# Closing stage of a four-layer graph network: GpSimd arithmetic removed from the last loop, statistics kept in SBUF, weights folded and five batches loaded while the last batch ends

## The chip, the core and the metric

The kernel runs on one core of a Trainium2 chip. The metric is device microseconds for one launch: the median of three runs of the kernel before is 2222.99 us (2221.63 to 2226.77). A core has five engines with a queue each: TensorE (PE, matrix products; its weight loads are shown as PEld), VectorE (DVE), ScalarE (ACT), GpSimd (POOL) and SyncE (SP). An engine takes the instructions of its queue in order. DMA transfers are issued from the queues of SP, ACT and POOL; an issue holds its queue until what it waits for has come.

## The reference

Sixteen graphs (batches) of 1024 nodes with 64 channels, a 1024 x 1024 adjacency matrix each, go through four layers. Each layer ends in "add to the input, then normalise over the channels". Layers 0 to 2 are a graph convolution, a Chebyshev graph filter and a quantile aggregation over neighbours with a small perceptron. The stage that is changed belongs to layer 3:

```python
Hf = H.reshape(batch * l, c)
mean = Hf.mean(axis=0)
var = jnp.mean((Hf - mean) ** 2, axis=0)
Hn = ((Hf - mean) * jax.lax.rsqrt(var + BN_EPS) * gamma + beta).reshape(batch, l, c)
d = A.sum(axis=2)
A_norm = jnp.sqrt(d)[:, :, None] * A * jax.lax.rsqrt(d)[:, None, :]
A_hat = jnp.eye(l, dtype=A.dtype) - A_norm
X = Hn @ W + b
out = jnp.einsum('bij,bjo->bio', A_hat, X)
return jax.nn.leaky_relu(out, negative_slope=0.01)
...
x = _layernorm(x + _L3_gnn_ref(x, adj, L3_gnn_gamma, L3_gnn_beta, L3_gnn_W, L3_gnn_b), axis=-1)
```

The mean and the variance run over the nodes of all sixteen batches. So nothing of the last product with `W` can be finished before the last batch has its layer-2 output, and the kernel needs a closing loop over the batches.

## The kernel before

The main phase works on the sixteen batches as a software pipeline. Each batch is a set of Python generators (`rows_in`, `layers`, `lists`, `fetch`, `heads`, `sorts`, `ends`, `back`, `third`), each with a table of due times in `WHEN`, and a new batch starts every `PERIOD` (120) units. All steps are sorted by due time and emitted in that order under a manual schedule; so the order on every engine's queue is written out by hand, and the engines only wait for semaphores.

`third` is the last generator of a batch. Its step "again" loads the transposed adjacency back (four transfers of 1 MB). Its step "u" (index 1) turns the layer-2 output `f_x3t` on PE, copies it on ACT (L1006), stores it to DRAM (`x3_d`, L1007), takes the batch-norm statistics on DVE (L1009) and stores those to DRAM in two small transfers (`st_d`, L1011), then scales by 1/sqrt(degree) on ACT (L1014, L1015). Its step "sum" is the product with the adjacency (`hop2`, L464: 16 matmuls of fp32, 32 passes on PE). The last two steps scale, subtract and store the result `z` (`z_d`, L1038).

After the main phase a flag is computed (L1083 to L1088): was there any node for which the fast path is not valid? Every engine loads the flag into a register (L1092) and branches (L1094) past a fallback that computes all batches in another way. The fallback is not taken with these inputs. The branch target is the closing stage.

The closing stage first folds: it loads the statistics of all batches from DRAM (`sts`, L1645) and gamma, beta, `W` and bias (L1647 to L1654), aggregates (L1656), forms 1/sqrt(var + eps) on ACT (L1658) and a small matrix `left` on DVE, multiplies it with `W` on PE (L1674), and writes the result twice into a block-diagonal matrix `w_2` (L1681). Then the closing loop treats each batch in seven steps, again under a manual schedule, with a lag in batches for each step:

```python
for t in range(-2, B + 3):
    for step, late in ((centre, 2), (finish, 3), (residual, 1), (square, 2), (mean, 1), (root, 2), (product, -2)):
        if 0 <= t - late < B:
            step(t - late)
```

`product` loads `z` (SP queue) and `x3` (ACT queue), 256 KB each, and multiplies `z` with `w_2` (L1694). `residual` is the leaky rectifier (ACT L1700, DVE L1701), the residual addition (DVE L1703) and the sum over channels (DVE L1705). `centre` subtracts the mean on POOL (L1713), `square` squares on ACT and sums on DVE (L1717, L1719), `root` is a square root on ACT (L1723), `finish` a reciprocal on DVE (L1727), a product on POOL (L1729) and the store of the batch's output from SP (L1730).

Of the kernel before, what the change touches and what calls it, by code (L numbers as in the profile page):

```python
# [218 lines left out]
def gnn_layers_kernel(  # L219
# [64 lines left out]
    st_d = dpool.tile([B, C, 12], F32, name="st_d")  # L284
# [41 lines left out]
    flag_i = cpool.tile([P, 1], I32, name="flag_i")  # L326
    stack = ExitStack()
# [484 lines left out]
    def heads(b, st, gots, pw, ps_):  # L812

        meta, xs = st["meta"], st["xs"]
        for ns, nr, _, ks in CLASSES:
# [38 lines left out]
            home = ps_.tile([P, HOME], F32, name="home", bufs=2)[:, 0 : ns * nk * C].rearrange(  # L854
# [141 lines left out]
    def third(b, st, pa, pw):  # L996
# [11 lines left out]
        st = pw.tile([P, 6], F32, name="f_st")  # L1008
        nc.vector.bn_stats(out=st, in_=xt)  # L1009
        for h in range(2):  # L1010
            nc.sync.dma_start(out=st_d[b][:, h * 6 : h * 6 + 6], in_=st[h * C : (h + 1) * C, :])  # L1011
# [27 lines left out]
        yield "z"  # L1039

    with (
# [23 lines left out]
        for b in range(B):  # L1065
            st = {}
            for name, part in (
                ("rows in", rows_in(b, st, keyband, pa, pw)),
                ("layers", layers(b, st, pw)),
                ("lists", lists(b, st, pw)),  # L1070
                ("fetch", fetch(b, st, gots)),
                ("heads", heads(b, st, gots, pw, ps_)),
                ("sorts", sorts(b, st, ps_)),
                ("ends", ends(b, st, pw)),
                ("back", back(b, st, pw)),
                ("third", third(b, st, pa, pw)),
            ):
                parts += [(b * PERIOD + when, b, name, u, part) for u, when in enumerate(WHEN[name])]
        for _, b, name, u, part in sorted(parts, key=lambda p: p[0]):
            next(part)  # L1080

        most = fc.tile([P, 1], F32, name="most")
        nc.vector.tensor_reduce(out=most, in_=missed, axis=AX.XY, op=ALU.max)  # L1083
        most_h = fc.tile([P, 1], BF16, name="most_h")
        nc.vector.tensor_scalar(out=most_h, in0=most, scalar1=0.0, scalar2=None, op0=ALU.is_gt)
        ps = bank("end")
        nc.tensor.matmul(ps[:, 0:1], lhsT=ones_h, rhs=most_h, start=True, stop=True)
        nc.vector.tensor_scalar(out=flag_i, in0=ps[:, 0:1], scalar1=0.0, scalar2=None, op0=ALU.is_gt)  # L1088
# [4 lines left out]
    with (  # L1093
# [40 lines left out]
        with tc.For_i(0, B, 1) as b:  # L1134
# [128 lines left out]
            with (  # L1263
                tc.tile_pool(name="l2", bufs=1) as l2,
                tc.tile_pool(name="l2d", bufs=2) as l2d,
# [315 lines left out]
            with tc.tile_pool(name="post", bufs=1) as post:  # L1581
# [34 lines left out]
                nc.sync.dma_start(out=st_d[bass.ds(b, 1)].rearrange("o c s -> c (o s)"), in_=st.rearrange("c f s -> c (f s)"))  # L1616
# [26 lines left out]
    with tc.tile_pool(name="fin1", bufs=1) as fin1, tc.tile_pool(name="fin", bufs=4) as fin, tc.tile_pool(name="ps_small", bufs=6, space=PSUM) as psum["small"]:  # L1643
        sts = fin1.tile([C, B, 12], F32, name="sts")
        nc.sync.dma_start(out=sts, in_=st_d.rearrange("b c s -> c b s"))  # L1645
        gam = fin1.tile([C, 2], F32, name="gam")
        nc.scalar.dma_start(out=gam[:, 0:1], in_=gamma.rearrange("(c o) -> c o", o=1))  # L1647
        nc.scalar.dma_start(out=gam[:, 1:2], in_=beta.rearrange("(c o) -> c o", o=1))
        w3_s = fin1.tile([C, C], F32, name="w3_s")
        nc.scalar.dma_start(out=w3_s, in_=w3)  # L1650
        b3_s = fin1.tile([P, C], F32, name="b3_s")
        nc.vector.memset(b3_s, 0.0)
        for h in range(2):
            nc.scalar.dma_start(out=b3_s[h * C + C - 1 : h * C + C, :], in_=b3.rearrange("(o c) -> o c", o=1))  # L1654
        mv = fin1.tile([C, 2], F32, name="mv")
        nc.vector.bn_aggr(out=mv, in_=sts.rearrange("c b s -> c (b s)"))  # L1656
        rs = fin1.tile([C, 1], F32, name="rs")
        nc.scalar.activation(rs, mv[:, 1:2], AF.Sqrt, bias=eps_s[0:C, :], scale=1.0)  # L1658
        nc.vector.reciprocal(rs, rs)
        nc.vector.tensor_tensor(out=rs, in0=rs, in1=gam[:, 0:1], op=ALU.mult)  # L1660

        left = fin1.tile([C, P], F32, name="left")
        shifts = fin1.tile([C, 1], F32, name="shifts")
        nc.vector.tensor_tensor(out=shifts, in0=mv[:, 0:1], in1=rs, op=ALU.mult)
        nc.vector.tensor_tensor(out=shifts, in0=gam[:, 1:2], in1=shifts, op=ALU.subtract)
        for h in range(2):
            cols = slice(h * C, (h + 1) * C)
            nc.vector.tensor_tensor(
                out=left[:, cols], in0=ident[0:C, 0:C], in1=ident[0:C, C - 1 : C].to_broadcast([C, C]), op=ALU.subtract
            )  # L1670
            nc.vector.tensor_scalar(out=left[:, cols], in0=left[:, cols], scalar1=rs, scalar2=None, op0=ALU.mult)
            nc.vector.tensor_copy(out=left[:, h * C + C - 1 : h * C + C], in_=shifts)
        ps = small()
        nc.tensor.matmul(ps[:, 0:C], lhsT=left, rhs=w3_s, start=True, stop=True)  # L1674

        w_2 = fin1.tile([P, P], F32, name="w_2")
        nc.vector.memset(w_2, 0.0)
        nc.vector.tensor_tensor(out=b3_s, in0=ps[:, 0:C], in1=b3_s, op=ALU.add)
        for h in range(2):
            hp = slice(h * C, (h + 1) * C)  # L1680
            nc.vector.tensor_scalar(out=w_2[hp, hp], in0=b3_s[hp], scalar1=-1.0, scalar2=None, op0=ALU.mult)  # L1681

# [3 lines left out]
        def product(b):  # L1686
            z = fin.tile([P, 512], F32, name="zf")
            nc.sync.dma_start(out=z, in_=z_d[b])  # L1688
            x3 = fin.tile([P, NK, C], F32, name="x3f", bufs=6)
            nc.scalar.dma_start(out=x3, in_=x3_d[b].rearrange("p (k c) -> p k c", c=C))  # L1690
# [4 lines left out]
            st[b].update(ps=ps, x3=x3)  # L1695

        def residual(b):
            psv = st[b]["ps"].rearrange("p (k c) -> p k c", c=C)
            low = fin.tile([P, NK, C], F32, name="low")
            nc.scalar.activation(low, psv, AF.Copy, scale=0.01)  # L1700
            nc.vector.tensor_tensor(out=psv, in0=low, in1=psv, op=ALU.max)  # L1701
            h = fin.tile([P, NK, C], F32, name="hf")
            nc.vector.tensor_tensor(out=h, in0=psv, in1=st[b]["x3"], op=ALU.add)  # L1703
            s = fin.tile([P, NK], F32, name="s")
            nc.vector.tensor_reduce(out=s, in_=h, axis=AX.X, op=ALU.add)  # L1705
            st[b].update(h=h, s=s)

        def mean(b):
            nc.scalar.mul(st[b]["s"], st[b]["s"], -1.0 / C)

        def centre(b):
            h, s = st[b]["h"], st[b]["s"]
            nc.gpsimd.tensor_tensor(out=h, in0=h, in1=s.unsqueeze(2).to_broadcast(wide), op=ALU.add)  # L1713

        def square(b):
            q = fin.tile([P, NK, C], F32, name="qf")
            nc.scalar.activation(q, st[b]["h"], AF.Square)  # L1717
            v = fin.tile([P, NK], F32, name="v")
            nc.vector.tensor_reduce(out=v, in_=q, axis=AX.X, op=ALU.add)  # L1719
# [5 lines left out]
        def finish(b):  # L1725
            r = fin.tile([P, NK], F32, name="r")
            nc.vector.reciprocal(r, st[b]["v"])  # L1727
            y = fin.tile([P, NK, C], F32, name="yf")
# [38 lines left out]
```

## Time and profile before

| | |
|---|---|
| three runs | 2226.77, 2222.99, 2221.63 us; median 2222.99 |
| profiled execution, its own time | 2229.29 us |
| its span, first to last instruction | 2227.4 us |
| mean granted TensorE clock | 0.871 |
| busy in the span | PE 1671.2 us (75%), DVE 1864.1 us (84%), ACT 1484.5 us (67%), POOL 1734.7 us (78%) |
| product with the adjacency of the last batch begins | 2126.60 us |
| last `z` copied (ACT L1037) | 2140.86 us, 0.59 us long |
| first product of the closing loop | 2154.60 us |
| last store of the output issued | 2221.65 us |
| engines at work after 2147 us | DVE 49.15, POOL 32.73, PE 30.51, ACT 26.50 of 80 us |

All times in the text are counted from the first instruction of this span. A line of the timeline gives the start, the duration, the engine, the line of the kernel and the operation, then the shapes, and in brackets how long the engine had been idle and what ended that. A "q" after an engine's name means its instruction queue: DMA issues, branches and waits. Busy shares over the whole span say little here, since all of the change lies in the last 100 us and in one step per batch before them.

### The profile page before, as it was taken

The page shows a single profiled execution, that of the slowest core. Times are in us where ns is not written, and L with a number is a line of the kernel's source. Part 1 is how long each engine was busy: PE and PEld are TensorE (multiplying, and loading weights), DVE is VectorE, ACT ScalarE, POOL GpSimd, SP SyncE. Part 2 cuts the span into 40 slices and gives each one's busy share as a digit, 9 for nine tenths or more (in the row PEclk, how much of TensorE's full clock was granted, in tenths as well). Part 3 has the DMA queues.
Part 4 walks back from the last instruction along what each step waited for, and adds up shares of the span by engine and source line. Part 5 has one row for each costly group of instructions (what it writes and reads, how often), then busy time and mean ns, then how long its engine had stood idle before and what let it go on. Part 6 is the DMA issues. An engine that isn't in the chain of part 4 may idle for free. (4 is left out here: it accounts for less than half of the span.)

```text
span 2227.4 us, 35713 instructions
## 1 busy us (share of the span) xinstructions
PE 1671.2 (75%) x9926; PEld 935.9 (42%) x9926; DVE 1864.1 (84%) x5687; ACT 1484.5 (67%) x5397; POOL 1734.7 (78%) x2279
## 2 busy tenths in 40 slices
PE   4876788878788778878788778878787877755653
PEld 3443444444445344444435344444444443333333
DVE  7658989889898989989898989999998988677536
ACT  3544767768686767768685767768686766675523
POOL 0078989899989989978787978889888979888014
PEclk9988889889899999989899998989998988876675
DMA  4444253533435353533535353533435352231226
GB/s 148 167 112 130 72 186 92 167 97 109 155 87 177 92 194 82 173 98 99 161 87 174 91 193 83 174 96 118 145 85 181 97 183 75 57 105 26 82 81 158
DMA packets 130481, 272.42 MB, mean 122 GB/s; under 512 B 77025, under 2 KB 77281, under 8 KB 120033
## 3 DMA queue, kind: packets, MB, share of 16 engines
q1 hardware_dynamic: 57536, 218.90, 27.2%
q0 software_dynamic: 35840, 37.92, 10.4%
q10 hardware_dynamic: 36896, 13.23, 2.4%
q8 instruction: 80, 1.31, 0.2%
q14 instruction: 129, 1.05, 0.2%
HBM read 185.89 MB, written 84.07 MB: 121 GB/s over the span
## 5 line engine op out<-in xcount | busy, mean ns | idle before, releaser
L803 POOL DMA_INDIRECT got<-rows,ids x1072 | 1139.7, 1063 | 186.0 <-issue 125.0
L806 POOL MEMSET rest<- 128x384 f32 x1120 | 509.4, 455 | 0.6
L464 PE MATMUL ps_l<-f_adj_t,f_t 128*64 128x512 f32 x1536 | 359.0, 622 | 35.5 <-ACT f_t L603 35.5
L875 ACT ACTIVATE home<-got,big 128x64 f32<-128x64 f32 x1344 | 329.9, 334 | 0.0
L907 DVE TENSOR_TENSOR away<-home 128x768 f32<-128x768 f32 (+9 forms) x416 | 228.9, 572 | 43.6 <-PE ps_xt L924 34.5
L924 PE MATMUL ps_xt<-home,quarter 128*128 128x256 f32 (+2 forms) x672 | 199.1, 404 | 65.0 <-ACT home L923 58.5
L923 ACT ACTIVATE home<-home,wts 128x64 f32<-128x64 f32 x896 | 226.8, 336 | 2.2 <-DVE home L907 2.0
L464 PEld LDWEIGHTS ps_l<-f_adj_t,f_t 128*64 128x64 f32 x1536 | 110.3, 142 | 250.7 <-issue 207.3
L539 DVE MAX8 cand<-key 128x8 f16<-128x128 f16 x1024 | 210.6, 278 | 4.4
L803 POOL DMA_INDIRECT extra<-rows,more x48 | 50.8, 1058 | 177.0 <-ACT row L780 116.1
L534 ACT ACTIVATE key<-f_a 128x1024 f16<-128x1024 f32 x128 | 135.0, 1055 | 59.2 <-DVE cand L539 42.1
L489 PE MATMUL ps_turn<-cf,f_a 128*128 128x128 f32 x1024 | 149.2, 293 | 31.2 <-ACT f_adj_t L490 18.1
L907 DVE TENSOR_TENSOR home<-away,home 128x128 f32<-128x128 f32 (+5 forms) x352 | 166.4, 473 | 6.2
L924 PEld LDWEIGHTS ps_xt<-home,quarter 128*128 128x128 f32 x672 | 110.5, 214 | 139.6 <-ACT home L923 139.5
L490 ACT COPY f_adj_t<-ps_turn 128x512 f32<-128x512 f32 x256 | 135.7, 582 | 39.3 <-PE ps_turn L489 39.3
L489 PEld LDWEIGHTS ps_turn<-cf,f_a 128*128 128x128 f32 x1024 | 120.4, 149 | 79.8 <-issue 47.6
L907 DVE TENSOR_TENSOR home<-away 128x64 f32<-128x64 f32 (+7 forms) x304 | 149.7, 510 | 1.1
L536 DVE TENSOR_TENSOR key<-key,keyband 128x1024 f16<-128x1024 f16 x128 | 87.6, 685 | 53.8 <-ACT key L534 53.8
L464 PE MATMUL ps_end<-f_adj_t,f_u 128*64 128x512 f32 x512 | 124.2, 641 | 8.9 <-ACT f_u L1015 8.9
L924 PE MATMUL ps_xt<-away,quarter 128*128 128x64 f32 (+1 forms) x448 | 94.9, 340 | 47.4 <-ACT away L923 46.8
L510 PE MATMUL ps_end<-at,f_h 128*64 128x512 f16 x256 | 62.3, 464 | 85.6 <-DVE at L988 85.5
L907 DVE TENSOR_TENSOR home<-home 128x64 f32<-128x64 f32 (+7 forms) x240 | 120.1, 500 | 7.2
(248 smaller groups left out, 3472.4 us busy)
## 6 DMA issues: line engine op xcount, KB each, us to landing
f_a<-in_adj_dram SPq DMA_DIRECT2D x128, 512.0 KB, 3.6
adj<-f_adj_t SPq DMA_DIRECT2D x16, 4096.0 KB
f_adj_t<-adj SPq DMA_DIRECT2D x64, 1024.0 KB, 22.2
got<-rows,ids POOLq DMA_INDIRECT x1072
rows<-xr ACTq DMA_DIRECT2D x16, 264.0 KB, 17.1
f_x<-in_x_dram ACTq DMA_DIRECT2D x16, 256.0 KB, 5.3
x_d<-f_x SPq DMA_DIRECT2D x16, 256.0 KB
z_d<-f_ht SPq DMA_DIRECT2D x16, 256.0 KB
```

The lines of the kernel that those rows point to most:

```text
L464: nc.tensor.matmul(ps[h * C : (h + 1) * C, :], lhsT=v[:, j, :], rhs=pairs[:, j, h], start=(j == 0), stop=(j == NK - 1),)
L489: nc.tensor.transpose(pt[:, j * P : (j + 1) * P], a[:, (4 * g + j) * P : (4 * g + j + 1) * P], ident)
L490: nc.scalar.copy(adj_t[:, 4 * g : 4 * g + 4, i * P : (i + 1) * P], pt.rearrange("p (j n) -> p j n", n=P))
L534: nc.scalar.activation(flat_key, a, AF.Sign)
L536: nc.vector.tensor_tensor(out=flat_key, in0=flat_key, in1=keyband[:, off : off + N], op=ALU.mult)
L539: nc.vector.max(out=cand[:, i, j * 8 : j * 8 + 8], in_=key[:, j, :])
L803: nc.gpsimd.indirect_dma_start(out=w[0], out_offset=None, in_=rows[:, :], in_offset=bass.IndirectOffsetOnAxis(ap=w[1], axis=0))
L806: nc.gpsimd.memset(rest, 0.0)
L875: nc.scalar.activation(home[:, s + 1, k, :], got[:, s, k, 0:C], AF.Identity, bias=big_dead[:, s, k : k + 1], scale=1.0,)
L907: nc.vector.tensor_tensor(out=at(ho, r1 if is_max else r0, *run), in0=at(ha, r0, *run), in1=at(hb, r1, *run), op=ALU.max if is_max else AL ...
L923: nc.scalar.mul(t[:, k, :], t[:, k, :], wts[:, i, k : k + 1])
L924: nc.tensor.matmul(total, lhsT=quarter, rhs=flat(t), start=False, stop=(i == nr - 1))
```

## The change

- The statistics of a batch stay in an SBUF tile `stats` (128 partitions x 16 x 6), written by the statistics instruction itself; the two small stores to DRAM and the load of `sts` fall away. The two halves of the partitions hold even and odd node blocks and are merged with two small matmuls in `fold`.
- `flag` is emitted after the last step of `lists` for the last batch. It runs through the PSUM bank `px`.
- `ahead` is emitted after step "again" of `third` for the last batch: it loads `z` and `x3` of batches 0 to 4 into the two row buffers `home`, ten transfers of 256 KB on the SP queue, behind the loads of the adjacency and ahead of the last batch's stores. `home` now comes from a pool `ph` that outlives the main phase.
- `fold_in` is emitted after step "u" of `third` for the last batch, so before its step "sum": five small loads on the ACT queue, some 20 small DVE instructions, one square root on ACT, three matmuls on PE (L1072, L1073, L1090 of the changed file).
- The closing loop has no POOL instruction. `centre` is one DVE instruction (scalar_tensor_tensor) that also multiplies the sum by -1/64, so the `mean` step on ACT falls away; the last scaling is eight ACT multiplications per batch; `x3` is loaded from the SP queue behind `z`. The rectifier writes to SBUF in place. The steps have new lags.
- In the fallback (not taken) a pool has one buffer less, and the loads and the fold are made again.

```diff
...
     z_d = dpool.tile([B, P, 512], F32, name="z_d")
-    st_d = dpool.tile([B, C, 12], F32, name="st_d")
...
+    stats = cpool.tile([P, B, 6], F32, name="stats")
+    w_2 = cpool.tile([P, P], F32, name="w_2")
+    nc.vector.memset(w_2, 0.0)
+    ph = ctx.enter_context(tc.tile_pool(name="f_home", bufs=2))
...
-        nc.vector.bn_stats(out=st, in_=xt)
-        for h in range(2):
-            nc.sync.dma_start(out=st_d[b][:, h * 6 : h * 6 + 6], in_=st[h * C : (h + 1) * C, :])
+        nc.vector.bn_stats(out=stats[:, b, :], in_=xt)
...
+    early = {}
+
+    def fill():
+
+        for b, (z, x3) in early.items():
+            nc.sync.dma_start(out=z, in_=z_d[b])
+            nc.sync.dma_start(out=x3, in_=x3_d[b])
+
+    def fold_loads(t):
+
+        gam, w3_s, b3_s = t[0:C, 0:2], t[0:C, C : 2 * C], t[:, 2 * C : 3 * C]
+        nc.scalar.dma_start(out=gam[:, 0:1], in_=gamma.rearrange("(c o) -> c o", o=1))
+        nc.scalar.dma_start(out=gam[:, 1:2], in_=beta.rearrange("(c o) -> c o", o=1))
+        nc.scalar.dma_start(out=w3_s, in_=w3)
+        nc.vector.memset(b3_s, 0.0)
+        for h in range(2):
+            nc.scalar.dma_start(out=b3_s[h * C + C - 1 : h * C + C, :], in_=b3.rearrange("(o c) -> o c", o=1))
...
+    def fold(params, ps):
...
+        nc.vector.bn_aggr(out=mv, in_=stats.rearrange("p b s -> p (b s)"))
+        nc.tensor.matmul(ps[0:C, 0:2], lhsT=halves[:, 0:C], rhs=mv, start=True, stop=True)
+        nc.tensor.matmul(ps[0:C, 2:4], lhsT=halves[:, C : 2 * C], rhs=mv, start=True, stop=True)
+        mean, apart = two[:, 0:1], two[:, 1:2]
+        nc.vector.tensor_copy(out=two, in_=ps[0:C, 0:4:2])
...
+        nc.scalar.activation(rs, var, AF.Sqrt, bias=eps_s[0:C, :], scale=1.0)
+        nc.vector.reciprocal(rs, rs)
...
+        nc.tensor.matmul(ps[:, C : 2 * C], lhsT=left, rhs=w3_s, start=True, stop=True)
+        nc.vector.tensor_tensor(out=b3_s, in0=ps[:, C : 2 * C], in1=b3_s, op=ALU.add)
+        for h in range(2):
+            hp = slice(h * C, (h + 1) * C)
+            nc.vector.tensor_scalar(out=w_2[hp, hp], in0=b3_s[hp], scalar1=-1.0, scalar2=None, op0=ALU.mult)
...
+        def flag():
...
+            ps = bank("px")
+            nc.tensor.matmul(ps[:, 0:1], lhsT=ones_h, rhs=most_h, start=True, stop=True)
+            nc.vector.tensor_scalar(out=flag_i, in0=ps[:, 0:1], scalar1=0.0, scalar2=None, op0=ALU.is_gt)
+
+        def ahead():
+            room = [ph.tile([P, HOME], F32, name="home") for _ in range(2)]
+            room = [t[:, u : u + 512] for t in room for u in range(0, HOME - 511, 512)]
+            for b in range(len(room) // 2):
+                early[b] = room[2 * b], room[2 * b + 1]
+            fill()
+
+        def fold_in():
+            params = fold_loads(pw.tile([P, 512], F32, name="f_t", bufs=2))
+            fold(params, bank("l1"))
+
+        last = {("lists", 14): flag, ("third", 0): ahead, ("third", 1): fold_in}
         for _, b, name, u, part in sorted(parts, key=lambda p: p[0]):
             next(part)
...
+            if b == B - 1 and (name, u) in last:
+                last[name, u]()
...
         def product(b):
-            z = fin.tile([P, 512], F32, name="zf")
-            nc.sync.dma_start(out=z, in_=z_d[b])
-            x3 = fin.tile([P, NK, C], F32, name="x3f", bufs=6)
-            nc.scalar.dma_start(out=x3, in_=x3_d[b].rearrange("p (k c) -> p k c", c=C))
+            z, x3 = early.get(b) or (fin.tile([P, 512], F32, name="zf"), fin.tile([P, 512], F32, name="x3f", bufs=6))
+            if b not in early:
+                nc.sync.dma_start(out=z, in_=z_d[b])
+                nc.sync.dma_start(out=x3, in_=x3_d[b])
             ps = psum["small"].tile([P, 512], F32, tag="small", name="psf")
...
+        def low(b):
+            h = fin.tile([P, NK, C], F32, name="hf")
+            nc.scalar.activation(flat(h), st[b]["ps"], AF.Copy, scale=0.01)
+            st[b].update(h=h)
+
+        def leaky(b):
+            h = flat(st[b]["h"])
+            nc.vector.tensor_tensor(out=h, in0=h, in1=st[b]["ps"], op=ALU.max)
...
-        def mean(b):
-            nc.scalar.mul(st[b]["s"], st[b]["s"], -1.0 / C)
...
         def centre(b):
             h, s = st[b]["h"], st[b]["s"]
-            nc.gpsimd.tensor_tensor(out=h, in0=h, in1=s.unsqueeze(2).to_broadcast(wide), op=ALU.add)
+            nc.vector.scalar_tensor_tensor(
+                out=h, in0=s.unsqueeze(2).to_broadcast(wide), scalar=-1.0 / C, in1=h, op0=ALU.mult, op1=ALU.add
+            )
...
+        def inverse(b):
             r = fin.tile([P, NK], F32, name="r")
             nc.vector.reciprocal(r, st[b]["v"])
+            st[b].update(r=r)
+
+        def finish(b):
+            h, r = st[b]["h"], st[b]["r"]
             y = fin.tile([P, NK, C], F32, name="yf")
-            nc.gpsimd.tensor_tensor(out=y, in0=st[b]["h"], in1=r.unsqueeze(2).to_broadcast(wide), op=ALU.mult)
+            for k in range(NK):
+                nc.scalar.mul(y[:, k, :], h[:, k, :], r[:, k : k + 1])
             nc.sync.dma_start(out=out[b].rearrange("(k p) c -> p k c", p=P), in_=y)
 
         with tc.manual_schedule():
-            for t in range(-2, B + 3):
-                for step, late in ((centre, 2), (finish, 3), (residual, 1), (square, 2), (mean, 1), (root, 2), (product, -2)):
+            for t in range(-4, B + 1):
+                for step, late in (
+                    (low, -2), (centre, 0), (inverse, 1), (leaky, -1), (square, 0), (spread, 0),
+                    (residual, -1), (finish, 1), (root, 0), (product, -4),
+                ):
                     if 0 <= t - late < B:
                         step(t - late)
```

`residual` keeps the addition and the sum over channels; the sum of squares of `square` is now a step of its own, `spread`.

## The prediction

> **What bounds the kernel now.** I read the page first, for the share of each engine in time; then two stretches, the last batch alone and the closing loop; then the timeline of each; then the chain of waits inside the loop. The page says 84% for DVE and 78% for POOL over the whole span, but the edits lie in the last 100 us. The stretches from 2078 to 2147 and from 2147 to 2227 us (columns: length, then busy time and instructions of PE, PEld, DVE, ACT, POOL, then clock, DMA share, GB/s):
>
> ```profile
> 2078.00:2147.00 69.00, 42.74 (x166) 23.09 (x166) 18.53 (x35) 29.79 (x116) 0.00 (x0) 0.67 0.19 73
> 2147.00:2227.00 80.00, 30.51 (x130) 27.21 (x130) 49.15 (x96) 26.50 (x65) 32.73 (x32) 0.54 0.61 159
> ```
>
> In the first, one batch is left and no engine is busy for two thirds of it: it is a chain, one engine after another, and anything put into that chain adds in full. In the second, DVE is busy for 49 of 80 us, so DVE does not bind either; a loop of waits does. The chain at the end of the first stretch and the start of the second (timeline: start, duration, engine, line):
>
> ```profile
> 2124.30 2.02 ACT L1014 ACTIVATE f_u<-f_x,f_rd 128x64 f32<-128x64 f32 x8
> 2126.34 0.20 ACT L1015 COPY f_u<-f_rd 128x8 f32<-128x8 f32 x1
> 2126.60 8.42 PE L464 MATMUL ps_end<-f_adj_t,f_u 128*64 128x512 f32 x32 [2.96 <-ACT f_u L1015]
> 2140.86 0.59 ACT L1037 COPY f_ht<-ps_end 128x512 f32<-128x512 f32 x1 [2.65 <-PE ps_end L1035]
> 2141.47 0.34 SPq L1038 DMA_DIRECT2D z_d<-f_ht  x1
> 2147.34 0.49 ACTq L1647 DMA_DIRECT2D gam<-in_L_gnn_gamma_dram  x1
> 2147.87 1.05 ACTq L1648 DMA_DIRECT2D gam<-in_L_gnn_beta_dram  x1
> 2148.96 0.61 ACTq L1650 DMA_DIRECT2D w_s<-in_L_gnn_W_dram  x1
> 2149.66 1.19 ACTq L1654 DMA_DIRECT2D b_s<-in_L_gnn_b_dram  x2
> 2151.56 0.29 ACT L1658 ACTIVATE rs<-mv,eps_s 64x1 f32<-64x1 f32 x1 [10.12 <-DMA w_s<-in_L_gnn_W_dram]
> 2154.60 2.72 PE L1694 MATMUL psf<-w,zf 128*128 128x128 f32 x11 [0.74 <-DVE w L1681]
> ```
>
> The reader is to see two things: the product with the adjacency starts 0.06 us after ACT's last small copy, so whatever ACT or PE does ahead of it delays it; and 13.15 us pass from the end of the `z` copy (2141.45) to the first product of the loop (2154.60). Then one period of the loop:
>
> ```profile
> 2172.70 0.40 SPq L1730 DMA_DIRECT2D out_dram<-yf  x1
> 2173.20 0.52 SPq L1688 DMA_DIRECT2D zf<-z_d  x1
> 2175.39 0.60 ACT L1700 ACTIVATE low<-psf 128x512 f32<-128x512 f32 x1 [0.20 <-ACT v L1723]
> 2176.01 0.70 DVE L1701 TENSOR_TENSOR psf<-low,psf 128x512 f32<-128x512 f32 x1 [0.59 <-ACT low L1700]
> 2176.43 2.05 PE L1694 MATMUL psf<-w,zf 128*128 128x128 f32 x8 [1.71 <-DMA zf<-z_d]
> 2176.80 0.69 DVE L1703 TENSOR_TENSOR hf<-psf,x3f 128x512 f32<-128x512 f32 x1
> 2177.53 0.69 DVE L1705 TENSOR_REDUCE s<-hf 128x8 f32<-128x512 f32 x1
> 2178.13 0.68 DVE L1719 TENSOR_REDUCE v<-qf 128x8 f32<-128x512 f32 x1
> 2179.34 0.60 ACT L1700 ACTIVATE low<-psf 128x512 f32<-128x512 f32 x1 [0.20 <-ACT v L1723]
> ```
>
> The period is 3.95 us (2175.39 to 2179.34), a ring: `low` .60, rectifier, addition, sum, sum of squares on DVE, root on ACT, next `low`. A `z` load starts PE 3.23 us after its issue (2173.20 to 2176.43) and the product is done at 2178.48. That product is not needed at once: `low` of a batch comes 10.4 us after the store that its load is queued behind, 4.6 us more than the 5.8 from that store's issue (2172.70) to the product's end.
>
> **The change, part by part.**
>
> *Flag and statistics.* The flag leaves the end; its chain there (copy end 2141.45 to flag 2141.85) is part of the 13.15 us. In its new place near 1968 us its PE and DVE steps may hold DVE by 0.7 to 1.3 us, once. POOL's gathers set the pace of that stage until 2066, and DVE itself waits for PE there, so I take 0, bounds 0 to 1.3. Two small stores per batch go from SP (1.11 us of SP per batch, row `st_d` at 2124.72); nobody waits for SP there: 0.
>
> *Early loads.* Ten transfers on SP, after the last adjacency loads and ahead of two stores. The row buffers come free by 2095; 2.6 MB at the 170 GB/s that busy slices show is 15 us at most, over well ahead of the store issued at 2124.29. The cover is the idle DMA (share 0.19). Cost 0; a gain is counted below.
>
> *Fold ahead of the last adjacency product.* ACT is free at 2126.36 and then issues five loads: by the rows above 0.49, about 0.5 (1.05 with SP issuing too), 0.61, and 1.19 for two, 2.6 to 2.9 us with gaps, 3.5 as shown contended. I take 2.75, as SP is quiet here. Then the root 0.3, DVE's chain from there to `left` (in the trace 2151.89 to 2152.99) 1.1 plus hand-overs and two shared small steps, 1.6 to 1.8 by that row's spacing, then PE's product of `left` 0.44 to 0.67. PE takes these in order, so the adjacency product starts at 2126.36 + 2.75 + 0.33 + 1.7 + 0.55 = 2131.7 in place of 2126.60: 5.1 later, with 0.3 for four hand-overs between engines 5.4. PE has then idled some 8 us instead of 3: behind 5.93 us of idle the same product took 9.05 us for the batch before (at 2057.06), against 8.42 here, which adds 0.6. Sum +6.0; bounds +4.4 (loads at 0.4 each, no clock loss) to +8 (contended issues, waits for the weights' landing). Everything to the `z` copy moves with it.
>
> *From the `z` copy to the first product.* Left are the `z` issue 0.36, the branch 3.84 (PE's row on the page reads 3762 ns for it, SP reached its target 3.84 after the flag was in), and SP's semaphore catch-up 0.55: 4.8. Saved: 13.15 - 4.8 = 8.35. `z` of batches 0 to 4 is in SBUF, so nothing waits for DMA there. The engines' own loads of the flag run beside SP's issue.
>
> *The loop.* DVE now has six instructions of 128x512 or a small one per batch: rectifier .70, addition .70, sum .69, centring, sum of squares .68 and the reciprocal .20. With the starts in the trace (0.61 apart where independent, 0.72 where one needs the other) one pass is .70 + .03 + .63 + .03 + .59 + .73 + .72 = 3.43. The centring (scalar_tensor_tensor over 128x512) has no row; the nearest are the tensor_tensor over the same tile, 0.69 to 0.70, and POOL's 1.04. I take 0.70, as it is DVE's own and reads as much. ACT per batch: .49 + .52 + eight scalings 2.01 (row L1014) + .30 = 3.3, below DVE.
>
> The Trainium skill ("Vector Engine (DVE) Microarchitecture Reference", section "7. Points that are easy to get wrong") says that this instruction with two non-bf16 SBUF sources runs at half throughput. No row here shows it at this size; by the rule it would be an estimated 1.24 us, the pass 3.97 and the whole forecast 2.2 us later.
>
> The `z` loads decide. In the new order `z` of batch t+4 is issued behind the store of batch t-1, and `low` needs it two turns later, ahead of the scalings on ACT that end in store t+1. That is a ring over two batches: .03 + store .48 + load 3.24 + product 2.05 + .08 + `low` .49 + square .52 + scalings 2.01 = 8.90, so 4.45 per batch. It beats the DVE pass (2 x 3.43 = 6.86), and the 3.95 of before: the slack of 4.6 us is gone. First output: product 2.05, `low`, rectifier, addition, sum, centring to 5.67, a pass to 9.10, scalings to 11.66; then six rings, 53.4; then two passes and the last turn, 3.43 + 3.43 + 2.47 = 9.33. First product to last store: 74.4. Before it was 67.05 (2154.60 to 2221.65). Cost +7.35.
>
> *The tail.* The last store landed at 2224.22 and SP was done at 2224.67, but POOL drained until 2226.7:
>
> ```profile
> 2221.65 0.37 SPq L1730 DMA_DIRECT2D out_dram<-yf  x1
> L1763 POOLq DRAIN  x3: 45/113/6062, 2220.6 to 2227.2; - x3
> ```
>
> Its drain, 6.06 us from 2220.55, comes behind its last product. With no POOL work it is over long before; the end is then the store's landing and 0.74: 3.76 after the last issue in place of 5.8. Saved 2.04; nothing saved if the drain still starts last.
>
> *Sum.* +6.0 - 8.35 + 7.35 - 2.04 = +2.96. On the profiled execution's own 2229.29 (span 2227.4) that is 2232.3; that execution lies 6.3 above the median of the runs, so against 2222.99 I say 2226.0, or +0.13%. Below 0.2% (4.4 us) a measurement of this kernel can't tell a change from none.
>
> **The rivals.**
>
> *The `z` load is in time, faster.* If load and product together took 3.25 us instead of 5.29, the ring would fall to 6.86 and DVE's pass of 3.43 would set the period: 11.66 + 14 x 3.43 + 2.47 = 62.2, 4.85 less than before. The sum is +6.0 - 8.35 - 4.85 - 2.04 = -9.2, 2213.8; with the fold's lower bound 2212.2. For it: PE's eight passes could run at a higher clock (the first products took 0.25 us a pass, these too). Against it: eleven loads of the trace all took 3.1 to 3.3 us from issue to PE.
>
> *The three transfers of a batch crowd one queue, slower.* Store, `z` and `x3` are now all on SP; `x3` was on ACT's. Each 0.1 us in the ring costs 0.6 in all, so from 0.25 us more, the change is measurably slower; at 4.8 us for a landing, which is what the crowded first loads show, the ring is 1.57 longer: +9.4, 2235. For it: 0.5 of SP per issue. Against it: the order store, then `z` is the same as in the rows above, and `x3` comes behind.
>
> *The fold costs nothing.* If ACT's issues ran ahead, beside the scalings, or PE did the adjacency product first, +6.0 falls away: 2220.0. Against it: PE's queue has the three fold products ahead of it and ACT's issues sit behind L1015.
>
> *The drain stays, or the store's landing is later:* +2.0, 2228.
>
> **How the numbers follow.** The main case, ring and fold as summed, 0.70: its own range is 2219 to 2231, from the fold's bounds (-1.6 to +2) and the ring's (0.3 either way, 2 us), the flag and the tail's; of it 0.40 lies within 0.2%, 0.28 above, 0.02 below. `z` in time: 0.13, faster, nearly all. Fold hidden: 0.04, within or just faster. Crowded queue, or the centring at its dear end: 0.13, slower. So faster 0.17, same 0.43, slower 0.40. The range is to leave out 2 in 10: from 2213, where half of the fast case is in, to 2234, the near end of the crowded one.
>
> **What would show it.** Right: the last adjacency product 5 to 6 us later after the five ACT issues; 4.8 us from `z` copy to first product; `z`-waiting PE and ACT idle before `low` in every second batch, outputs 8.9 us apart in pairs; POOL's drain early. Wrong: `low` waiting on DVE or on nothing, outputs evenly 3.4 apart (fast case); `zf` 4 us and more from issue to PE (slow case); the centring at 1.0 or more.

## The result and the profile after

The changed kernel takes 2233.35 us (median of eight runs, 2229.06 to 2236.85) against 2223.82 for the kernel before (eight runs). The ratio is 1.0044, with a 95% interval of 1.0029 to 1.0059: slower, by 6 to 13 us. The changed kernel was timed a second time, beside variants: 2231.06 against 2226.24, ratio 1.0020 (1.0005 to 1.0034). The two intervals share 1.0029 to 1.0034, or 6.4 to 7.6 us. The forecast was 2226.0, with a range of 2213 to 2234.

The two profiled executions differ by 7.1 us (2234.5 against 2227.4). Cut at the marks that the prediction used, from the start times and durations in the two timelines:

| stretch | before | after | difference |
|---|---|---|---|
| start to batch 13's layer-2 output (ACT, copy to `f_x3t`) | 1958.07 | 1957.68 | -0.4 |
| from there to batch 14's | 91.77 | 93.36 | +1.6 |
| from there to batch 15's | 72.50 | 73.97 | +1.5 |
| to the start of the last adjacency product | 4.26 | 9.52 | +5.26 |
| that product | 8.42 | 9.35 | +0.93 |
| its end to the end of the `z` copy | 6.43 | 5.89 | -0.54 |
| `z` copy to the first product of the loop | 13.16 | 4.24 | -8.92 |
| first product to the issue of the last store | 67.05 | 76.11 | +9.06 |
| that issue to the end | 5.80 | 4.36 | -1.44 |

The outputs of batches 13, 14 and 15, on which the first rows rest, before:

```profile
1958.07 0.56 ACT L992 COPY f_x3t<-ps_end 128x512 f32<-128x512 f32 x1
...
2049.84 0.57 ACT L992 COPY f_x3t<-ps_end 128x512 f32<-128x512 f32 x1
...
2122.34 0.59 ACT L992 COPY f_x3t<-ps_end 128x512 f32<-128x512 f32 x1 [9.39 <-PE ps_end L510]
```

and after:

```profile
1957.68 0.56 ACT L995 COPY f_x3t<-ps_end 128x512 f32<-128x512 f32 x1
...
2051.04 0.56 ACT L995 COPY f_x3t<-ps_end 128x512 f32<-128x512 f32 x1
...
2125.01 0.59 ACT L995 COPY f_x3t<-ps_end 128x512 f32<-128x512 f32 x1 [9.63 <-PE ps_end L513]
```

The timeline of the changed kernel around the fold shows the fourth to the seventh row of the table:

```profile
2126.96 2.02 ACT L1014 ACTIVATE f_u<-f_x,f_rd 128x64 f32<-128x64 f32 x8
...
2129.01 0.20 ACT L1015 COPY f_u<-f_rd 128x8 f32<-128x8 f32 x1
2129.02 0.48 ACTq L1052 DMA_DIRECT2D f_t<-in_L_gnn_gamma_dram  x1
2129.54 0.61 ACTq L1053 DMA_DIRECT2D f_t<-in_L_gnn_beta_dram  x1
2130.19 0.61 ACTq L1054 DMA_DIRECT2D f_t<-in_L_gnn_W_dram  x1
2130.89 0.69 ACTq L1057 DMA_DIRECT2D f_t<-in_L_gnn_b_dram  x2
2131.63 0.29 ACT L1078 ACTIVATE f_t<-f_t,eps_s 64x1 f32<-64x1 f32 x1 [2.42 <-DMA f_t<-in_L_gnn_beta_dram]
...
2133.92 0.69 PE L1090 MATMUL ps_l<-f_t 64*128 64x64 f32 x2 [5.98 <-DVE f_t L1089]
2134.53 9.35 PE L467 MATMUL ps_end<-f_adj_t,f_u 128*64 128x512 f32 x32
...
2149.18 0.59 ACT L1037 COPY f_ht<-ps_end 128x512 f32<-128x512 f32 x1 [2.11 <-PE ps_end L1035]
2149.80 0.34 SPq L1038 DMA_DIRECT2D z_d<-f_ht  x1
2154.01 7.38 PE L1732 MATMUL psf<-w,home 128*128 128x128 f32 x40 [4.86 <-SPq L1164]
```

The adjacency product (L467) starts 5.32 us after the end of ACT's copy L1015, where it was 0.06, and what stands between are the five issues, the root, DVE's chain and the fold's product, in the order that was forecast. After the `z` copy there is nothing but the store's issue, the branch and waits for semaphores. In the loop, the timeline of one ring of two batches reads:

```profile
2174.89 0.39 SPq L1780 DMA_DIRECT2D out_dram<-yf  x1
...
2175.33 0.58 SPq L1727 DMA_DIRECT2D zf<-z_d  x1
...
2178.32 0.40 SPq L1780 DMA_DIRECT2D out_dram<-yf  x1
...
2179.07 2.05 PE L1732 MATMUL psf<-w,zf 128*128 128x128 f32 x8 [3.92 <-DMA zf<-z_d]
...
2181.21 0.60 ACT L1737 ACTIVATE hf<-psf 128x512 f32<-128x512 f32 x1 [2.72 <-PE psf L1732]
```

PE waits for the `z` load, ACT's `low` (now L1737) waits for the product, and stores come in pairs: 3.4 to 3.7 us apart, then 5.2 to 6.2. The groups of the loop, with the idle time of the engine ahead of each, say the same in sums:

```profile
L1732 PE MATMUL psf<-w,zf 128*128 128x128 f32 x88 | 22.5, 437 | 33.8 <-DMA zf<-z_d 29.3 <-DVE r L1772 4.5
...
L1753 DVE SCALAR_TENSOR_TENSOR hf<-s,hf 128x512 f32<-128x512 f32 x16 | 11.1, 691 | 0.6
L1764 DVE TENSOR_REDUCE v<-qf 128x8 f32<-128x512 f32 x16 | 11.0, 687 | 15.0 <-ACT qf L1759 14.8
...
L1737 ACT ACTIVATE hf<-psf 128x512 f32<-128x512 f32 x16 | 9.5, 593 | 24.1 <-PE psf L1732 24.1
```

ACT lost 24.1 us ahead of `low` and DVE 14.8 ahead of the sum of squares. The new centring instruction (L1753) takes 0.69 us.

### The profile page after: what moved, and what is told of

The parts are those of the page before. It is cut to its first block, busy times and chain, and to the rows that moved or that the text cites. A ratio compares the mean times of both kernels' runs of the same rounds, so it can differ in the third digit from the quotient of the medians.

```text
span 2234.5 us, 35726 instructions
## 1 busy us (share of the span) xinstructions
PE 1672.3 (75%) x9930; PEld 938.6 (42%) x9930; DVE 1872.8 (84%) x5709; ACT 1510.0 (68%) x5509; POOL 1700.3 (76%) x2247
## 3 DMA queue, kind: packets, MB, share of 16 engines
q14 instruction: 129, 1.06, 0.1%
## 5 line engine op out<-in xcount | busy, mean ns | idle before, releaser
L467 PE MATMUL ps_l<-f_adj_t,f_t 128*64 128x512 f32 x1536 | 359.9, 623 | 35.5 <-ACT f_t L606 28.0
L467 PEld LDWEIGHTS ps_l<-f_adj_t,f_t 128*64 128x64 f32 x1536 | 110.5, 143 | 251.3 <-issue 209.0
L539 DVE TENSOR_TENSOR key<-key,keyband 128x1024 f16<-128x1024 f16 x128 | 87.6, 685 | 53.4 <-ACT key L537 49.8
L467 PE MATMUL ps_end<-f_adj_t,f_u 128*64 128x512 f32 x512 | 127.1, 654 | 5.9 <-ACT f_u L1015 5.9
```

The costliest lines, as they stand in the source:

```text
L467: nc.tensor.matmul(ps[h * C : (h + 1) * C, :], lhsT=v[:, j, :], rhs=pairs[:, j, h], start=(j == 0), stop=(j == NK - 1),)
L539: nc.vector.tensor_tensor(out=flat_key, in0=flat_key, in1=keyband[:, off : off + N], op=ALU.mult)
```

## The experiments

Each kernel is the changed one with the edit shown. Ratios are to the kernel before, run on the same chip.

**The loads of the loop one turn earlier (e1_z_earlier).**

```diff
-            for t in range(-4, B + 1):
+            for t in range(-5, B + 1):
...
-                    (residual, -1), (finish, 1), (root, 0), (product, -4),
+                    (residual, -1), (finish, 1), (root, 0), (product, -5),
```

> The changed kernel with one edit: the closing loop issues the loads and the product of a batch one turn earlier (lag -5 in place of -4). Theory (the z load closes a ring over two batches, 8.9 us and more, and this costs the loop): the same ring now spans three batches, 8.9/3 = 2.97 a batch, under the DVE pass of 3.43; so ACT's low waits for no product, the stores are 3.4 apart, first product to last store issue falls from 76.1 to about 62.2 us, and the time falls by 13.9, to about 2219.5. Rival (DMA binds: store, z and x3 are 768 KB a batch, which in 3.43 us is 229 GB/s, above the 194 of the loop of before): the period stays near 3.9 to 4.0, the loads come later still, and the gain is 6 to 8, about 2226. Rival (the loop is not what cost): within 2 us of 2233.4.

Measured: 2218.29 us, ratio 0.9979 (0.9964 to 0.9994): faster than the kernel before. First product to last store issue: 62.43 us (forecast 62.2, 76.11 in the changed kernel). SP's timeline in the middle of the loop:

```profile
2178.38 0.40 SPq L1780 DMA_DIRECT2D out_dram<-yf  x1
2178.87 0.53 SPq L1727 DMA_DIRECT2D zf<-z_d  x1
2179.49 0.46 SPq L1728 DMA_DIRECT2D x3f<-x_d  x1
2181.81 0.39 SPq L1780 DMA_DIRECT2D out_dram<-yf  x1
...
2185.24 0.40 SPq L1780 DMA_DIRECT2D out_dram<-yf  x1
```

Every store follows the one ahead of it by 3.43 us, which is the DVE pass. The rival "DMA binds" falls: 768 KB in 3.43 us went through. The ten `z` loads in the steady loop took 3.3 to 4.2 us from issue to PE, no less than in the changed kernel; with one more turn to land in, that cost nothing. So two numbers in the order of steps, and not the work, made the loop of the changed kernel 9 us longer than the loop before.

**The fold beside the adjacency product (e2_fold_beside).** The small loads go to SP behind the early loads; `fold` stops ahead of its last product, and goes on when the adjacency product has been emitted.

```diff
-        nc.scalar.dma_start(out=w3_s, in_=w3)
+        nc.sync.dma_start(out=w3_s, in_=w3)
...
+        yield
         nc.tensor.matmul(ps[:, C : 2 * C], lhsT=left, rhs=w3_s, start=True, stop=True)
...
-        last = {("lists", 14): flag, ("third", 0): ahead, ("third", 1): fold_in}
+        last = {("lists", 14): flag, ("third", 0): ahead, ("third", 1): fold_in, ("third", 2): fold_out}
```

> The changed kernel with the fold taken off the chain of the last batch: its five small loads are issued from SP behind the ten early loads, and its last product (of left with W) stands behind the adjacency product of the last batch, not ahead. Theory: the adjacency product starts within 0.5 us of ACT's copy L1015 again (some 5.3 us sooner) and is some 0.5 to 0.9 shorter, as PE has idled less; the time falls by 5.5 to 6.2, to about 2227.5. Rival (the clock or the rest of the main phase, not the fold, is what came later): less than 3 us gained.

Measured: 2224.15 us, ratio 0.9998 (0.9984 to 1.0012). The timeline:

```profile
2130.21 0.20 ACT L1015 COPY f_u<-f_rd 128x8 f32<-128x8 f32 x1
2130.31 0.29 ACT L1078 ACTIVATE f_t<-f_t,eps_s 64x1 f32<-64x1 f32 x1
...
2130.46 1.12 PE L467 MATMUL ps_end<-f_adj_t,f_u 128*64 128x512 f32 x2 [1.35 <-ACT f_u L1015]
```

The adjacency product starts 0.05 us after the copy again, and takes 8.63 us in place of 9.35: 5.27 + 0.72 = 6.0 us of the trace, as the theory had it. Against the two measurements of the changed kernel, which did not run beside this one, it is 6.9 and 9.2 between the medians, and 4.9 and 10.2 by the ratios to the kernel before.

**Both edits (e3_both).**

> Both edits together. Theory: the two causes lie one after another, so their gains add: 13.9 + 5.8 = 19.7, about 2213.7, 10 us under the kernel before. If DMA binds the loop: about 2220. If a rest of some 5 us sits in the main phase of the changed kernel, it is still there, and would show as the last batch's layer-2 output later than in the kernel before.

Measured: 2210.69 us, ratio 0.9931 (0.9915 to 0.9948). The adjacency product starts 0.05 us behind the copy, the loop takes 62.42 us: both gains are there in full, side by side. This is 13 us under the kernel before by the medians and 15 by the ratio, so the parts of the change are worth having; two places in its order were not.

**The old loop behind the new front (e4_old_loop).** The loop of the kernel before, with POOL, behind the changed flag, statistics, early loads and fold. The core of the edit:

```diff
-        with tc.manual_schedule():
-            for t in range(-4, B + 1):
...
+            for t in range(-2, B + 3):
+                for step, late in ((centre, 2), (finish, 3), (residual, 1), (square, 2), (mean, 1), (root, 2), (product, -2)):
```

> The changed kernel up to its closing loop (flag, statistics, early loads and fold as changed), with the closing loop of the kernel before: centring and last scaling on POOL, mean on ACT, x3 from ACT, lags as before; z and x3 of batches 0 to 4 from the row buffers. Theory: the loop takes 66 to 67 us in place of 76.1, POOL's drain is back at the end (1.3 to 2 us), so the time falls by 7 to 8.5, to about 2225.5: the front part alone is then worth +2 against the kernel before: -8.9 to the first product, +5.7 by the fold, and a rest of about 5 in the main phase. Rival (no rest in the main phase, the medians differ by chance): about 2220.5, 3 under the kernel before.

Measured: 2225.54 us, ratio 1.0003 (0.9985 to 1.0021), with a loop of 66.78 us and 5.80 from the last store's issue to the end. So the new loop in its new order costs some 9 us and gives 1.4 at the end, and the front part alone comes out even: the interval, 3 us less to 5 us more, holds the theory (2 more) and the rival (3 less), and the time alone does not choose between them.

**Where the rest sits.** The table of stretches leaves 3.1 us in batches 13 to 15, which the prediction had at nothing. In the nine traces with an unmoved flag (two of the changed kernel and seven of variants, this section's later ones too), batch 14's output follows batch 13's by 93.3 to 93.5 us (91.8 before), and batch 15's follows that by 74.0 to 74.1 (72.5 before). Earlier batches drift: by batch 12 the traces lie between 12 us ahead of the one of before and 1 behind it. These last steps don't. The timeline of the changed kernel there:

```profile
1965.27 0.96 DVE L910 TENSOR_TENSOR home<-home 128x768 f32<-128x768 f32 x1
...
1966.14 0.28 DVE L1136 TENSOR_REDUCE most<-missed 128x1 f32<-128x128 f32 x1
1966.45 0.16 DVE L1138 TENSOR_SCALAR most_h<-most 128x1 bf16<-128x1 f32 x1
1966.52 0.59 ACT L785 COPY xs<-ps_px 128x512 f32<-128x512 f32 x1 [1.21 <-PE ps_px L479]
1967.15 0.16 PE L1140 MATMUL ps_px<-most_h,ones_h 128*128 128x1 bf16 x1 [0.67 <-ACT xs L785]
1967.25 3.68 PE L467 MATMUL ps_end<-f_adj_t,f_u 128*64 128x512 f32 x8
1967.35 0.16 DVE L1141 TENSOR_SCALAR flag_i<-ps_px 128x1 int32<-128x1 f32 x1 [0.74 <-PE ps_px L1140]
1967.43 0.68 DVE L910 TENSOR_TENSOR home<-away 128x512 f32<-128x512 f32 x1
```

and in the kernel before, without the flag:

```profile
1966.54 0.68 DVE L907 TENSOR_TENSOR home<-away 128x512 f32<-128x512 f32 x1
1966.80 3.39 PE L464 MATMUL ps_end<-f_adj_t,f_u 128*64 128x512 f32 x10
```

The flag's matmul waits until ACT has emptied the bank `px`, and batch 13's adjacency product is behind it in PE's queue: that product starts 9.56 us after batch 13's output, against 8.73 before, and DVE's next step comes 1.28 us later. Then single passes of that product ran slower (1.06 us where 0.59 stood; the granted clock over the product was 0.75, before 0.87), which took the delay on PE to 2.1. From 20 us behind batch 13's output on, DVE is about as late as PE, some 2 us.

**The flag ahead of the fold (e5_flag_late, e11_flag_late).** This kernel was timed twice.

```diff
-        last = {("lists", 14): flag, ("third", 0): ahead, ("third", 1): fold_in}
+        last = {("third", 0): ahead, ("third", 1): fold_in}
...
         def fold_in():
+            flag()
```

> The changed kernel with only the flag moved: from behind the last batch's last step of its lists to just ahead of the fold, where PE waits for ACT anyway. Theory (the flag is the rest in the main phase: DVE waits 0.74 us for its matmul at 1966 to 1967, and PE's queue has that matmul ahead of batch 13's adjacency product, which starts 0.84 us later and then meets a slower clock): the step from batch 13's layer-2 output to batch 14's falls from 93.4 back to 91.8 us. If the slower clock of batch 14's product (9.95 in place of 9.05) is an after-effect of that too, the step from 14 to 15 falls from 74.0 back to 72.5 as well and the time by 3.1, to about 2230.2. Rival (the second step is slowed by the ten early loads or by something else): only 1.6 gained, 2231.7, and the second step stays at 74. Rival (chance): both steps stay as they are.

Measured: 2224.93 us, ratio 0.9991 (0.9974 to 1.0009). The steps (batch 13's output to 14's, and 14's to 15's) are 92.9 and 74.0 us. Up to 79 us behind batch 13's output, PE's and DVE's instructions stand within 0.3 us of where the kernel before has them, so the flag's own delay is gone; then other matmuls run slower, and 1.1 us of lateness come in. The second step did not change. The median fell by more than this trace explains; so the unmoved and the moved kernel were timed once more, on the same chip:

> The changed kernel as it is, beside the next one on the same chip. Open is how much of the 9.5 us between the medians is the steps of the last 100 us and of batches 13 to 15 (4.4 and 3.1 us by the traces, 7.5 together), and how much is the drift of the earlier batches from one execution to the next, which in single traces so far ran from -12 to +2 us against the kernel before by batch 12, with the same instructions. Theory: a ratio of 1.002 to 1.005, with the loop at 75.5 to 76.2 us and the step from batch 13 to 14 at 93.4. If the earlier measurement was high by drift: 1.001 to 1.003.

> The changed kernel with the flag ahead of the fold once more, beside the unmoved one. Theory (the flag's old place costs 0.8 to 1.7 us of the step from batch 13 to 14, no more): 1 to 3 us under the unmoved one. Rival (it costs far more, as 2224.9 against 2233.4 on two chips would have it): 6 to 11 us under it.

Measured: the unmoved kernel 2231.06 us, ratio 1.0020 (1.0005 to 1.0034); the moved one 2227.24, ratio 0.9994 (0.9971 to 1.0017). The unmoved kernel's trace has the step at 93.35 us and the loop at 75.72, as expected. The two kernels are 3.8 us apart by the medians and 5.8 by the ratios, with intervals that overlap. That lies between the theory (1 to 3) and the rival (6 to 11), and neither is met; what the traces show of the flag's place is 1.6 us. In the moved kernel's execution the steps were 91.8 and 69.2 us. That the second one is shorter goes with the clock: in the 20 us from 2095 of the changed kernel and from 2091 of this one (both from 44 us after batch 14's output), the stretches read

```profile
2095.00:2115.00 20.00, 11.63 (x39) 7.96 (x40) 0.95 (x3) 10.51 (x43) 0.00 (x0) 0.50 0.29 98
```

and, with the flag late,

```profile
2091.00:2111.00 20.00, 9.82 (x50) 6.50 (x51) 3.56 (x7) 9.77 (x38) 0.00 (x0) 0.67 0.20 67
```

The granted clock was 0.50 in the one and 0.67 in the other, and the same matmul (L943) took 1.22 and 0.69 us. The kernel before has the slow stretch too, with 1.22 us for this matmul (L940 there):

```profile
2094.00:2114.00 20.00, 10.21 (x36) 6.97 (x36) 2.34 (x5) 9.76 (x38) 0.00 (x0) 0.50 0.00 1
```

So the slow stretch is not a price of the flag: of thirteen traces, eleven have it. The two without it have the flag late, and a third with the flag late has it. What decides on that is not shown by these runs.

**The early loads later (e9_loads_late).**

```diff
-            fill()
 
         def fold_in():
             params = fold_loads(pw.tile([P, 512], F32, name="f_t", bufs=2))
             fold(params, bank("l1"))
+            fill()
```

> The changed kernel with only the ten early loads moved: issued from SP behind the fold, around 2127, and not behind the adjacency loads around 2090. Theory (the flag and the clock behind it slow batches 13 to 15, the loads are hidden): the step from batch 14's layer-2 output to batch 15's stays at 74.0 us. Rival (the loads collide with the last batch's work): it falls towards 72.5. In both cases the first product of the loop follows the z copy as before, within 0.3 us, as 2.6 MB land in some 16 us, before 2147.

Measured, in one execution: 74.0 us, so the early loads at 2090 did not slow batch 15. `z` copy to first product was 4.07 us. But the fold got longer: the adjacency product started 6.97 us after the copy L1015 in place of 5.32, because DVE waited for the small loads. Four of the large ones (1 MB) had been issued from SP ahead of them, from 2119.3 on:

```profile
2120.95 0.48 ACTq L1052 DMA_DIRECT2D f_t<-in_L_gnn_gamma_dram  x1
...
2125.06 0.15 DVE L1080 TENSOR_TENSOR f_t<-f_t 64x1 f32<-64x1 f32 x1 [1.01 <-DMA f_t<-in_L_gnn_gamma_dram]
...
2126.10 0.15 DVE L1082 TENSOR_TENSOR f_t<-f_t 64x1 f32<-64x1 f32 x1 [0.71 <-DMA f_t<-in_L_gnn_beta_dram]
```

Gamma, 256 bytes, came 4.1 us after its issue; in the changed kernel DVE used it 3.1 us after its issue without a wait. From batch 15's output to the end of the `z` copy this execution took 26.0 us, against 24.8, so the place of the early loads in the change, well ahead, was the better one of the two.

**`x3` from ACT's queue (e6_x3_act).**

```diff
-                nc.sync.dma_start(out=x3, in_=x3_d[b])
+                nc.scalar.dma_start(out=x3, in_=x3_d[b])
```

> The changed kernel with only x3 of batches 5 to 15 loaded from the ACT queue again (there as the kernel before had it, between the steps of the loop), so that SP issues the store and z alone. Theory (the ring is longer than summed because three transfers of a batch follow each other on one queue: from z's issue to PE 3.46 us on average where the ring goes through, against 3.24): these go back to 3.2 to 3.3 and the loop from 76.1 to between 74.4 and 75. Rival (the extra is DMA traffic, whatever queue it comes from): 76 again, or longer by what ACT spends on issues, about 0.3 us each on an engine that the ring goes through, up to 2 us in all.

Measured, in one execution: a loop of 76.07 us, no gain. The six `z` loads that the ring goes through took 3.46 us on average from issue to PE, the same mean as in the changed kernel (3.40, with a loop of 75.72, in its second trace). The queue is not what lengthens them; that it is traffic as such was argued by the rival and is not shown apart.

**A POOL instruction at the very end (e7_pool_last).**

```diff
+            if b == B - 1:
+                nc.gpsimd.tensor_copy(out=fin.tile([P, 8], F32, name="pt"), in_=y[:, NK - 1, 0:8])
```

> The changed kernel with one small POOL copy (128x8) behind the last batch's scalings. Theory (POOL's drain takes some 6 us from POOL's last instruction, whatever that was, and sets the end): the last scaling ends at 76 us after the first product, the copy is over 0.2 later, the drain ends 6 us after that, and from the last store's issue to the end pass 6.5 to 7.1 us, not 4.4. Rival (the drain is long only behind much POOL work): 4.4 us as before.

Measured, in one execution: 6.06 us from the last store's issue to the end, in place of 4.36. The timeline's two last lines, and the line of POOL's drain (count, then least, median and most ns, then first and last start):

```profile
2219.53 0.37 SPq L1780 DMA_DIRECT2D out_dram<-yf  x1
2219.57 0.19 POOL L1782 COPY pt<-yf 128x8 f32<-128x8 f32 x1 [164.79 <-DMA out_dram<-yf]
```

```profile
L1818 POOLq DRAIN  x3: 45/113/5203, 2219.5 to 2225.3; - x3
```

One copy of 0.19 us costs 1.7 us at the end: a drain of 5.20 us starts with it, 5.0 of it after the copy is over. The theory had 6 and overstated the end by half a microsecond; the rival ("only behind much work") falls. In the changed kernel the same drain is there too, hidden behind the last batch, since POOL's last work is at 2064.9:

```profile
L1816 POOLq DRAIN  x3: 45/113/6337, 2064.0 to 2234.2; - x3
```

The drain's length (5.2 to 6.3 us) differs because its record starts before POOL's last instruction ends. From that end to the drain's end it is 4.99 us in each of four traces: behind a memset in the changed kernel, behind the product of 1.04 us in the kernel before and in `e4_old_loop`, and behind the copy of 0.19 us in this run.

**All three edits (e8_best).**

> All three edits together: loads of the loop one turn earlier, fold beside the adjacency product, flag ahead of the fold. Theory: 2210.7 less the gain of the flag's move, so 2207.6 if both steps of the main phase come back, 2209.1 if only the first does; first product to last store 62.4 us, as with the first edit alone.

Measured: 2208.14 us, ratio 0.9924 (0.9906 to 0.9941); the loop 62.45 us. It is the fastest here, 17 to 18 us under the kernel before (by ratio and by medians), though its step from `e3_both` (0.9931) is inside the intervals. The median lies inside the forecast of 2207.6 to 2209.1, but the profiled execution does not show the forecast's steps, and at 2200.88 us it is the fastest of the five. Its steps to batches 14 and 15 are 91.8 and 69.2 us, but the last adjacency product then took 10.03 us (8.63 in `e3_both`) and the stretch from there to the `z` copy 7.30 (5.88). The granted clock was 0.75 in the step to batch 15 (0.65 in `e3_both`), 0.70 in the product (0.82) and 0.77 behind it (1.00): of 4.9 us gained, 2.8 went back.

## Why the prediction was right, and where its sizes were off

The direction of each step that it priced held, and the largest one, the ring of the `z` load, was confirmed by taking it away. Yet the forecast of 3 us more was a third to two thirds of what came. The main case's own range ended at 2231. 2233.35 is inside the full range because that was stretched to 2234 for the crowded queue, while 3.1 of the 4.4 us that the sum lacks against the traces came from elsewhere; to that extent it is luck. Against the trace:

| step | forecast | measured | |
|---|---|---|---|
| flag, in batches 13 to 15 | 0 (0 to 1.3) | +3.1, of which 1.6 is shown to be the flag's | wrong |
| fold to the `z` copy | +6.0 | +5.65 | right |
| `z` copy to first product | -8.35 | -8.92 | right |
| loop | +7.35 | +9.06 | mechanism right, short by 1.7 |
| tail | -2.04 | -1.44 | mechanism right, 0.6 too good |
| sum | +2.96 | +7.4 | |

*The step that failed* is the flag: "POOL's gathers set the pace of that stage until 2066, and DVE itself waits for PE there, so I take 0". POOL did keep its pace: its last instruction of that stage comes 107.2 us after batch 13's output, 107.6 before. But batch 14's output is not behind POOL alone: it is behind PE, and the flag's matmul stood on PE's queue ahead of batch 13's adjacency product. DVE was held by 1.28 us, inside the bound of 1.3; the text did not ask what was queued behind the flag's matmul on PE. Which of the two holds would have been enough for the 1.6 us is not separated by a run, as moving the flag takes both away. Of the 3.1 us, 1.6 is this place (nine traces with it, none of the three without it at 93.3 or over; in one of them 1.1 came back, from slower matmuls well behind the flag's old place). The other 1.5 is in the step from batch 14 to 15, where the granted clock was 0.65 against 0.69 before; 0.9 of it is batch 14's adjacency product (9.94 us against 9.05, at 0.71 and 0.78). That this follows from the flag is not shown, since one of three traces without the flag there has it too, and two have a step faster than before. Its cause stays open.

*The fold* came out by its parts: issues 2.6 (forecast 2.75), chain of DVE 1.91 (1.7), PE 0.6, and a product longer by 0.93 (0.6) after the idle time; 0.54 came back in the last product's stretch. The doubt about contended issues did not arise; `e9_loads_late` shows that it would have, in another form, with the large loads beside it.

*The loop* needed 54.8 us for six rings, not 53.4, and 0.3 more to the first store. The loads on the ring took 3.23, 3.73, 3.97, 3.31, 3.24 and 3.30 us from issue to PE; the sum had 3.24 for each, and the difference is 1.3 us. The prediction said that all eleven such loads before had taken 3.1 to 3.3 us. Nine had; the one issued at 2185.10 took 4.56 and the next 3.40, and the mean was 3.35. So a spread that the sum left out was already there in the kernel before, with `x3` on ACT's queue. The 4.8 us of "the crowded first loads" is the median of the two landings that the trace has, and one of them is this load in the middle of the loop. The rival of a crowded queue was right in sign, and wrong on its cause, as `e6_x3_act` shows; what does lengthen single loads stays open. The rival "in time" did not come; `e1_z_earlier` is that rival, made by order: 62.4 us against 62.2 worked out.

*The centring* was taken at 0.70 from its nearest row, and measures 0.69. The rule that was weighed against it (the Trainium skill, "Vector Engine (DVE) Microarchitecture Reference", section "7. Points that are easy to get wrong") would have made it an estimated 1.24; no run here shows a halved rate at this size in fp32, and the measurement decides.

*The tail*: POOL's drain went, as forecast. SP was through with its waits 3.0 us after the last store's issue in both traces. But its next drain then ends only at 2233.6, half a microsecond later, with 0.83 us of hand-shakes behind it, where 0.74 and no such drain were summed. In the trace of before that drain came at once and lay inside POOL's; why it came later is not shown.

## What to carry to other kernels

When a loop is given a new order, count the ring of each load: from the store or slot that frees its issue, through the landing and its consumer, back to that store, divided by the batches that it spans. If that is above the busiest engine's pass, one more turn of prefetch can be worth more than instructions saved; here it was 13.7 us for two changed numbers. Work that is moved "into idle time" is to be followed on every queue that it enters: the fold and the flag both hurt through one small matmul that stood ahead of a large one, and both were free once they stood behind it, or where PE waits anyway.

## What the runs showed of the hardware that was not expected

- The same 32 passes of the adjacency product took 8.0 us at a granted clock of 0.88 and 10.1 us at 0.70, both in one trace (`e5_flag_late`, batches 13 and 14). In `e8_best` a faster stretch was followed by a slower one that took back over half of the gain. A gain of 1 to 2 us beside such products is to be looked for in several traces.
- 768 KB per 3.43 us (229 GB/s) of store and loads went through one issuing queue without slowing the loop (`e1_z_earlier`).
- A load of 256 bytes, issued when four loads of 256 KB had just been issued from another queue, landed 4.1 us after its issue (`e9_loads_late`); without them it was there in at most 3.1.
- POOL's drain ended 4.99 us after the end of its last instruction in four traces, whether that had taken 0.19 or 1.04 us; where POOL stopped early it cost nothing.
